# Loads of weights and context moved to one queue in the order of use, and a planner's figures redone, in a fused cross-attention and ternary feed-forward kernel

## The chip, the cores and the metric

The kernel runs on one core of a Trainium2 chip. The metric is the device time of one execution in microseconds (us). The engines are named as in the profile: PE (TensorE, with PEld for its weight loads), DVE (VectorE), ACT (ScalarE), POOL (GpSimd) and SP (SyncE, which here only issues DMAs). ACT can issue DMAs too, on a queue of its own. "ACTq" and "SPq" are the queue rows of the profile.

## The reference

```python
def xattn(query, key_value, mask, Wq, bq, Wk, bk, Wv, bv, Wo, bo):   # E=512, H=16, D=32
    Q, K, V = (each (. @ W.T + b), split in 16 heads of 32)
    scores = einsum('bqhd,bkhd->bhqk', Q, K) / sqrt(32)
    scores = where(mask == 0, -inf, scores)            # 77 keys per batch
    probs = softmax(scores)
    return einsum('bhqk,bkhd->bqhd', probs, V).reshape(B, Lq, E) @ Wo.T + bo

def ffn(x, w1, conv_w, conv_b, w2):                    # hidden 2048
    h = bit_linear(x, w1)        # x rounded to int8 per row, w to -1, 0, 1 by its mean |w|
    h = depthwise_conv1d(h, conv_w, conv_b)            # 3 taps along the sequence
    return bit_linear(silu(h), w2)

x = x + xattn(layernorm(x), ctx_1024, mask, ...)       # x: 4 x 2048 x 512 float32
x = x + ffn(layernorm(x), w1, conv_w, conv_b, w2)
```

## The kernel before

The 8192 rows of x are cut into 64 blocks of 128 rows. Two blocks make a pair, which shares its transposed input and its query products. For the feed-forward part the blocks are grouped into 18 tiles (`TILES`: two of 2 blocks, fourteen of 4, one of 3, one of 1).

**Start.** Wq, Wk, Wv and Wo (1 MB each), the transposed context (616 KB), the mask and the small columns are loaded into three buffers of the tag "y" (stage_A: wq and wv, stage_B: wk and mask, stage_C: wo and context). Wq and Wo are each split into two fp16 halves (a maximum on DVE, L436; high half on ACT, L441; low half on DVE, L446). The masked context gives keys (L525, first for batch 0, later for batches 1 to 3), the context gives values (L596). The value tiles (vx) lie in buffers of the tag "pr", which the exponentials use later; they are stored to DRAM (`vd`, L640), and the first batch's go to `vblk` by eleven small transfers (L665). W1 and w2 (4 MB each) are loaded in four pieces of 1 MB each (L751), summed for their mean (L756 on ACT, L761 on DVE), rounded (w_q, L781 and L783) and clipped to fp8. They reuse the three "y" buffers as stage_A to stage_C come free.

**One block.** Load x (L923), normalise (L853 to L879), split into two fp16 halves (hl: high half at L899 on ACT or L901 on POOL, low half at L930 on POOL), transpose by DMA (xT, L935). The query products (pq, L1212 to L1214) run per pair, a copy adds the bias (qT, L1222 on ACT). For each of four chunks of heads: scores (psc, L956, two PSUM buffers), maxima on DVE (L961), four exponentials on ACT (pr, L968). Per half of the heads: a cast (ph, L899), the low half on POOL (L993), a DMA transpose (prT, L997), value products (pa, L1005), scaling on DVE (L1022). Then the context is split and transposed (cT, L1058), multiplied by Wo (po, L1065 to L1070), added to x (xb, L1080), kept in DRAM, quantised and transposed (xqT, L1150).

**One tile.** For each of 16 chunks of the hidden width: product (ph, L1252), scaling (h, L1266, DVE), and the convolution's three taps. The middle tap is on ACT (L1277). A letter of `WHO[..]["conv"]` says who does the other two: "b" is both on DVE (L1292, into py and then into y), "c" is one on DVE and one on ACT plus POOL (ta at L1299, added at L1306), "d" is both on ACT plus POOL. SiLU follows on ACT (L1352), then maxima on DVE (L1357, L1393), then the rounding in pairs of chunks (gq, L1432, on POOL for "P" and on DVE for "D" in `WHO[..]["round"]`), the last product (pf, L1452), the residual (xr, L1462) and the store.

**The order.** All steps are given to a planner (`Plan.schedule`), which runs in Python before the kernel is built. Each step has an engine, a cost, a priority and, for DMAs, a latency and a time of service; the planner also reckons with eight DMA lanes, where each DMA waits for the one eight before it (`LANES`). The order that comes out is fixed for every engine at the end of the kernel (a chain of dependencies without semaphores), so every engine works strictly through its list. The figures of `O` and `LATER` are offsets in blocks that set the priorities, `PARTS` says at which block another set of figures and of `WHO` begins. In the order before, SP issues x of blocks 0 and 1, wq, wk, and ACT issues the columns, the context, the mask and wv; wo and bo follow on SP after the second transpose. All pieces of w1 and w2 are issued by ACT.

Of the kernel before, what the change touches and what calls it, by code (L numbers as in the profile page):

```python
# [17 lines left out]
I32 = mybir.dt.int32  # L18
# [6 lines left out]
P = 128  # L25
B, S, E = 4, 2048, 512
NK = 77
CK = B * NK
CG = (CK + P - 1) // P
H, D = 16, 32  # L30
# [40 lines left out]


O = {
    "first": -15.42, "pv": -17.5, "late": 1145.74, "w1": -8.83, "w2": 1.01, "k1": 5.45,
    "wo": -16.83, "bo": 1.54, "load": -3.75, "sa": -3.3, "na": 1.1, "hi": -8.89, "lo": -3.28,
    "xT": -3.9, "q": -1.76, "q_step": 0.36, "sc": -0.48, "sc_step": 0.02, "ph0": 0.05,
    "ph1": 0.92, "v0": -0.35, "v1": -3.13, "cx": 1.43, "o": 2.89, "n": 3.81, "xq": 3.53,
    "xb": -1.54, "h": 5.15, "s": 0.95, "p8": 0.63, "p8_step": 0.28, "f": 2.1,
}

LATER = [
    {"late": 958.43, "load": -3.97, "sa": -2.95, "na": 0.33, "hi": -7.55, "lo": -2.85,
     "xT": -3.83, "q": -1.75, "q_step": 0.42, "sc": -0.46, "sc_step": 0.0, "ph0": 0.04,
     "v0": -0.41, "v1": -1.84, "cx": 1.35, "o": 2.83, "n": 3.74, "xq": 3.23, "xb": -1.61,
     "h": 2.6, "p8": 0.62, "p8_step": 0.3, "f": 0.3},
    {"late": 1881.15, "load": -3.79, "sa": -2.94, "na": -1.29, "hi": -7.77, "lo": -2.51,
     "xT": -3.19, "q": -1.75, "q_step": 0.41, "sc": -0.49, "sc_step": 0.05, "ph1": 0.52,
     "v0": -0.87, "v1": -1.44, "cx": 1.53, "o": 2.82, "n": 3.92, "xq": 3.12, "xb": 1.12,
     "h": 4.4, "s": 0.99, "p8": 0.67, "p8_step": 0.32, "f": -0.11},
    {"late": 3023.22, "load": -3.22, "sa": -2.58, "na": -4.14, "hi": -7.03, "lo": -4.11,  # L90
     "xT": -2.17, "q": -1.66, "q_step": 0.39, "sc": -0.46, "sc_step": 0.12, "ph0": 0.17,
     "ph1": 1.1, "v0": 0.42, "v1": -0.26, "cx": 1.24, "o": 2.96, "n": 3.77, "xq": 3.89,
     "xb": -0.59, "h": 5.43, "s": 0.96, "p8": 1.12, "p8_step": 0.39, "f": -3.15},
]
SILU_ALL = False
COUPLE = False
# [6 lines left out]

PARTS = (12, 44, 54)
WHO = [
    {"sa": "D", "sf": "D", "xh": "A", "ch": "A", "ph": "AA", "q": "AAAA",
     "conv": "cbbbbbbbbbbbbcbb", "round": "PPPPPPPP"},
    {"sa": "D", "sf": "D", "xh": "P", "ch": "A", "ph": "AA", "q": "AAAA",  # L110
     "conv": "cbccbbcbbbbbbcbb", "round": "PPPPPPPP"},
    {"sa": "D", "sf": "D", "xh": "A", "ch": "A", "ph": "AA", "q": "AAAA",
     "conv": "cccbdbbbbbbbccbb", "round": "PPPPPPPP"},
    {"sa": "D", "sf": "D", "xh": "P", "ch": "A", "ph": "AA", "q": "ADAA",
     "conv": "ddbbbdcbbbbddcbb", "round": "PDPDPDPD"},
]


# [45 lines left out]
class Plan:  # L164
# [13 lines left out]
    def add(  # L178
        self, eng, cost, prio, uses, makes, fn, lock=False, table=None, lat=None, serve=0.0,
        delay=0.0, dmas=None,  # L180
    ):
        cost *= self.PACE.get(eng, 1.0)
        self.steps.append(
            Step(
                len(self.steps), eng, cost, prio, uses, makes, fn, lock, table,
                self.LAT[eng] if lat is None else lat, serve, delay,
                int(serve > 0) if dmas is None else dmas,
            )
        )
# [95 lines left out]
def xattn_bitffn_kernel(  # L285
# [15 lines left out]
    nc = tc.nc  # L301
# [24 lines left out]
    add = plan.add  # L326
# [34 lines left out]
    def square(name):  # L361

        s, i = {"wq": ("A", 0), "wv": ("A", 1), "wk": ("B", 0), "wo": ("C", 0)}[name]
        return st[s][:, EC * i : EC * i + EC]

    def tail(name, a, n):
        return flat(st[name])[:, EC * E + a : EC * E + a + n]
# [4 lines left out]
    def ctx_view():  # L372
        return by_chunk(tail("C", 0, EC * CK))

    def load_square(name, src, queue=nc.sync):
        queue.dma_start(out=square(name), in_=src.rearrange("(c p) o -> p c o", p=P))

    def load_ctx():
        nc.scalar.dma_start(out=small_in, in_=cols)
        nc.scalar.dma_start(out=ctx_view(), in_=ctxT.rearrange("(c p) k -> p c k", p=P))  # L380
        nc.scalar.dma_start(
            out=tail("B", 5 * CK, CK).bitcast(I32), in_=mask.partition_broadcast(P)
        )

    def load_o():
        nc.sync.dma_start(out=bo_f, in_=bo.partition_broadcast(P))
# [1 line left out]

    for s in "ABC":
        add("SP", 1, -41, [], {s: "y"}, partial(stage, s), lat=0)  # L390
    big = dict(lat=5000, serve=3000)
    add("SP", 450, -39.5, ["A"], {"wqd": None}, partial(load_square, "wq", wqT), **big)
    add("ACT", 1350, -39, ["B", "C"], {"ctxd": None}, load_ctx, dmas=3, **big)
    add(
        "ACT", 450, -37, ["A"], {"wv": None}, partial(load_square, "wv", wvT, nc.scalar),
        delay=1200, lat=4000, serve=3000,
    )
    add("SP", 450, -36.5, ["B"], {"wk": None}, partial(load_square, "wk", wkT), **big)
    add("SP", 900, -22, ["C", ("xTd", 1)], {"wo": None}, load_o, dmas=2, **big)


    p2 = {i: fixed([P, 1], F32, f"p2_{i}") for i in ("wq", "wo", "v")}
# [328 lines left out]
    def plan_ternary(dst, src, deq, name, prio):  # L731
# [9 lines left out]
            st[name, h] = new([P, G, TMAX], F32, "y", f"{name}_{h}")  # L741

        def load(i):
            h, k = divmod(i, 2)
            q = whole // 4
            if name == "w1":
                v = src[:, i * P : (i + 1) * P].rearrange("c p f -> p c f")
            else:
                v = src[i * E : (i + 1) * E].rearrange("(n p) f -> p n f", p=P)
            room = flat(st[name, h])[:, k * q : k * q + q]  # L750
            nc.scalar.dma_start(out=room.rearrange("p (c f) -> p c f", f=E), in_=v)  # L751

        def total(i):
            q = whole // 4
# [36 lines left out]
        for i in range(4):  # L791
            pr, w = prio + 0.3 * i, (name, i // 2)
            if i % 2 == 0:
                add("SP", 1, pr, W_GATE[name], {w: "y"}, partial(half, i // 2), lat=0)
            eng = "ACT" if (name, i) in SUM_ACT else "DVE"
            add(
                "ACT", 450, pr, [w], {(name, "l", i): None}, partial(load, i), lat=4000, serve=2500,
            )
            add(
                eng, 1890 if eng == "ACT" else 2195, pr, [w, (name, "l", i)],  # L800
                {(name, i, "t"): None}, partial(total, i),
            )
        add(
# [2 lines left out]
        )  # L806
        for i in range(whole // step):
            pr, q = prio + 1.3 + 0.1 * i, (name, "i", i)
            uses = [(name, "m"), (name, i * step * 2 // whole), (name, "l", i * step * 4 // whole)]
            eng, cost = ("ACT", 1050) if W_ROUND[name][i] == "A" else ("Pool", 1250)  # L810
            add(eng, cost, pr, uses, {q: "gq"}, partial(round_, i))
            add("DVE", 610, pr, [q], {(name, i, "q"): None}, partial(clip, i), lock=True)
# [99 lines left out]
    def plan_block(t):  # L912
# [25 lines left out]

        x, xn, hl, xT = (("x", t), ("xn", t), ("hl", t), ("xT", p))
        ahead = O["first"] + 0.3 * t if t < 2 else t  # L940
        early = -40 + 0.1 * t if t < 2 else t + O["load"]
        add("SP", 460, early, [], {x: "x"}, load, **LANDS["x"])
        both = pair.setdefault(p, {})
        plan_norm(
# [612 lines left out]
```

## Time and profile before

| what | value |
|---|---|
| time, median of 3 runs (lowest to highest) | 1199.87 us (1199.43 to 1202.67) |
| time of the profiled execution | 1198.85 us |
| its span, granted clock | 1197.0 us, 0.984 |
| busy PE / PEld / DVE / ACT / POOL | 1100.9 / 737.4 / 1075.2 / 951.0 / 955.6 us |
| DMA | 185.31 MB, mean 155 GB/s |
| queue q1 (issued by SP) | 173.49 MB |
| queue q10 (issued by ACT) | 10.27 MB |

The span is the profiled stretch from the first instruction to the last; the time of the execution is 1.85 us longer. Busy time counts an engine's instructions without register, branch, semaphore and DMA-issuing ones. In a row of a waits view the waiting line comes first, then the line that released it. A row of a timeline gives start and duration in us, then in brackets the idle time before it and what ended that.

### The profile page before, as it was taken

What the parts mean: (1) busy time and instruction counts of PE and PEld (TensorE: products, weight loads), DVE (VectorE), ACT (ScalarE), POOL (GpSimd) and SP (SyncE); (2) the same over time, 40 slices, a digit from 0 to 9 for tenths busy, and PEclk for the clock granted to TensorE, in tenths of its full rate; (3) what the DMA queues carried; (4) which work ended last, traced back from release to release, by engine and by line L of the source; (5) the groups of instructions that cost most, each with busy time, mean ns of one, the idle gap of its engine ahead of it and who ended that gap; (6) DMA issues with size and microseconds to landing.
All of it is one profiled execution on the core that took longest, in us unless ns stands there. A gap on an engine that the chain in (4) does not pass through costs nothing. (4 is left out here: it accounts for less than half of the span.)

```text
span 1197.0 us, 24157 instructions
## 1 busy us (share of the span) xinstructions
PE 1100.9 (92%) x8231; PEld 737.4 (62%) x8231; DVE 1075.2 (90%) x2380; ACT 951.0 (79%) x2124; POOL 955.6 (80%) x903
## 2 busy tenths in 40 slices
PE   4778889999999999999999999999999999997777
PEld 2455656766666676667676666666666766654333
DVE  4678789999999999999999999999999999899796
ACT  2478798888888888878888898979897988865563
POOL 4468759966978989797998889796989888788554
PEclk9889999999999999999999999999999999999899
DMA  7698986978676886858687777777686766651122
GB/s 229 168 288 164 194 183 151 195 137 177 117 168 135 168 188 143 173 127 185 138 174 164 175 159 167 156 147 163 150 171 154 169 133 154 131 145 54 40 71 88
DMA packets 396923, 185.31 MB, mean 155 GB/s; under 512 B 348107, under 2 KB 349259, under 8 KB 396799
## 3 DMA queue, kind: packets, MB, share of 16 engines
q1 hardware_dynamic: 391231, 173.49, 66.1%
q10 hardware_dynamic: 5568, 10.27, 2.6%
q8 instruction: 65, 1.06, 0.4%
q14 instruction: 59, 0.48, 0.1%
HBM read 64.97 MB, written 34.68 MB: 83 GB/s over the span
## 5 line engine op out<-in xcount | busy, mean ns | idle before, releaser
L1432 POOL TENSOR_TENSOR gq<-y,qsb 128x1024 f16<-128x1024 f32 (+3 forms) x132 | 289.6, 2212 | 10.0 <-ACT qsb L1410 5.3
L1252 PE MATMUL ph<-xqT,w1q 128*128 128x257 f16 (+3 forms) x2048 | 277.3, 276 | 15.0 <-DVE h L1266 12.7
L1277 ACT ACTIVATE py<-h,small_in 128x512 f32<-128x512 f32 (+3 forms) x270 | 202.5, 750 | 93.4 <-DVE y L1292 90.5
L968 ACT ACTIVATE pr<-psc,nmx 128x77 f32<-128x77 f32 x1024 | 245.7, 341 | 30.5 <-DVE nmx L961 27.0
L1452 PE MATMUL pf<-w2q,gq 128*128 128x512 fp8e4 x1024 | 260.5, 382 | 10.1 <-DVE xr L1462 5.7
L1252 PEld LDWEIGHTS <-w1q 128*128 128x128 fp8e4 x2048 | 199.2, 99 | 83.9 <-issue 32.1
L993 POOL TENSOR_TENSOR ph<-pr,ph 128x616 f16<-128x616 f32 x128 | 174.7, 1366 | 50.8 <-ACT ph L899 36.9
L1266 DVE TENSOR_TENSOR h<-ph,dqb 128x514 f32<-128x514 f32 (+3 forms) x288 | 180.2, 626 | 22.6 <-PE ph L1252 20.0
L1292 DVE SCALAR_TENSOR_TENSOR y<-h,small_in,py 128x512 f32<-128x512 f32 (+3 forms) x270 | 185.2, 686 | 1.9 <-ACT py L1277 1.0
L956 PE MATMUL psc<-kblk,qT 128*128 128x308 f32 x512 | 174.2, 437 | 11.4 <-ACT pr L968 10.7
L1306 POOL TENSOR_TENSOR y<-y,ta 128x512 f32<-128x512 f32 (+3 forms) x105 | 120.6, 1149 | 63.7 <-ACT ta L1299 36.6
L1452 PEld LDWEIGHTS <-gq 128*128 128x128 f16 x1024 | 98.0, 98 | 100.0 <-issue 14.6
L1357 DVE TENSOR_REDUCE mx<-y 128x256 f32<-128x2048 f32 (+2 forms) x66 | 146.0, 2213 | 11.8 <-ACT y L1352 11.6
L1212 PE MATMUL pq<-xT,wq_hi 128*128 128x256 f16 x512 | 142.1, 277 | 13.2 <-DMA xT<-hl 9.7
L1292 DVE SCALAR_TENSOR_TENSOR py<-h,small_in,py 128x512 f32<-128x512 f32 (+3 forms) x201 | 137.2, 682 | 8.7 <-ACT py L1277 8.2
L1213 PE MATMUL pq<-xT,wq_hi 128*128 128x256 f16 x512 | 142.2, 278 | 0.0
L1214 PE MATMUL pq<-xT,wq_lo 128*128 128x256 f16 x512 | 142.2, 278 | 0.0
L961 DVE TENSOR_REDUCE nmx<-psc 128x4 f32<-128x308 f32 x256 | 117.6, 468 | 13.1 <-PE psc L956 12.7
L1352 ACT ACTIVATE y<-y 128x2048 f32<-128x2048 f32 (+3 forms) x72 | 120.0, 1712 | 0.7 <-DVE y L1292 0.3
L956 PEld LDWEIGHTS psc<-kblk,qT 128*128 128x128 f32 x512 | 86.3, 191 | 41.3 <-ACT pr L968 23.8
L1005 PEld LDWEIGHTS <-prT 128*128 128x128 f16 (+1 forms) x1920 | 86.2, 98 | 37.2 <-DMA prT<-ph 18.1
L1005 PE MATMUL pa<-vblk,prT 128*128 128x66 f16 (+2 forms) x1920 | 92.4, 200 | 11.2 <-DMA prT<-ph 7.8
(158 smaller groups left out, 2022.2 us busy)
## 6 DMA issues: line engine op xcount, KB each, us to landing
x<-in_x SPq DMA_DIRECT2D x64, 256.0 KB
xb<-in_x SPq DMA_DIRECT2D x64, 256.0 KB
x<-xb SPq DMA_DIRECT2D x64, 256.0 KB
xr<-x SPq DMA_DIRECT2D x64, 256.0 KB
out<-xr SPq DMA_DIRECT2D x64, 256.0 KB
w<-in_w1T ACTq DMA_DIRECT2D x4, 1024.0 KB
w<-in_w2T ACTq DMA_DIRECT2D x4, 1024.0 KB
prT<-ph SPq DMA_TRANSPOSE x128
```

The costliest lines, as they stand in the source:

```text
L956: nc.tensor.matmul(psc, pair[p]["q", c][:, half], kb[:, c], start=True, stop=True)
L968: nc.scalar.activation(o["pr", c // 2][:, n : n + NK], o["psc", c][:, h], AF.Exp, bias=o["nmx", c][:, h : h + 1],)
L993: nc.gpsimd.tensor_tensor(ph[:, 1, :HR], o["pr", hf], ph[:, 0, :HR], ALU.subtract)
L1005: nc.tensor.matmul(pa[:, h0:h1], prT[:n, l + j], v[:, :, r], start=(j == 0 and i == 0), stop=(j == NS - 1 and i == 2), skip_group_check=True,)
L1213: nc.tensor.matmul(pq, hi[:, ic, os], xs[:, 1, ic], start=False, stop=False)
L1252: nc.tensor.matmul(ph[:, i, :WH], w1q[:, c, f * P : (f + 1) * P], xqT[:, c, c0 : c0 + WH], start=(c == 0), stop=(c == EC - 1),)
L1266: nc.vector.tensor_tensor(in_parts(s["h", f]), s["ph", f][:, :parts, :WH], in_parts(tile_a[a]["dqb"]), ALU.mult,)
L1277: nc.scalar.activation(dst, s["h", f][:, 1 : 1 + T], AF.Identity, bias=cb_sb[:, f : f + 1], scale=cw_sb[:, f, 1:2],)
L1292: nc.vector.scalar_tensor_tensor(ins[dst](), s["h", f][:, i : i + T], cw_sb[:, f, i : i + 1], ins[src](), ALU.mult, ALU.add,)
L1357: nc.vector.tensor_reduce(s["m", g][:, c0:c1], ys[g][:, :, c0:c1].rearrange("p c t i -> p t c i"), AX.XY, ALU.max, apply_absolute_value=True,)
L1432: engine.tensor_tensor(gq[u][:, :, :T], y, q, ALU.mult)
L1452: nc.tensor.matmul(s["po", k], gq[f // 2][:, f % 2, k * P : (k + 1) * P], w2q[:, f], start=(f == 0), stop=(f == HC - 1),)
```

## The change

Three things change. (1) Wq, the columns, the context, the mask, wk, wv and all pieces of w1 and w2 are issued by SP, in the order of their use; ACT issues no DMA any more. (2) W1 and w2 come in eight pieces of 512 KB each, where they came in four of 1 MB; the sums wait for two pieces, a rounding waits for one. (3) The planner's latencies for these loads, all offsets in `O` and `LATER`, the boundaries `PARTS` and the assignment `WHO` are new. In `WHO`, the first chunk of a tile goes from "c" to "d" in the first three parts, one rounding of the third part goes from POOL to DVE, the third part's high half of hl goes from ACT to POOL, and the last part's conv and round letters are arranged anew (as many chunks with DVE taps: 20 taps on DVE, four pair roundings on DVE).

```diff
-    "first": -15.42, "pv": -17.5, "late": 1145.74, "w1": -8.83, "w2": 1.01, "k1": 5.45,
-    "wo": -16.83, "bo": 1.54, "load": -3.75, ...
+    "first": -14.87, "pv": -18.61, "late": 1061.05, "w1": -8.76, "w2": -2.26, "k1": 3.07,
+    "wo": -12.87, "bo": -5.67, "load": -5.34, ...
...
-PARTS = (12, 44, 54)
+PARTS = (12, 48, 56)
 WHO = [
     {"sa": "D", "sf": "D", "xh": "A", "ch": "A", "ph": "AA", "q": "AAAA",
-     "conv": "cbbbbbbbbbbbbcbb", "round": "PPPPPPPP"},
+     "conv": "dbbbbbbbbbbbbcbb", "round": "PPPPPPPP"},
     {"sa": "D", "sf": "D", "xh": "P", "ch": "A", "ph": "AA", "q": "AAAA",
-     "conv": "cbccbbcbbbbbbcbb", "round": "PPPPPPPP"},
-    {"sa": "D", "sf": "D", "xh": "A", "ch": "A", "ph": "AA", "q": "AAAA",
-     "conv": "cccbdbbbbbbbccbb", "round": "PPPPPPPP"},
+     "conv": "dbccbbcbbbbbbcbb", "round": "PPPPPPPP"},
+    {"sa": "D", "sf": "D", "xh": "P", "ch": "A", "ph": "AA", "q": "AAAA",
+     "conv": "dccbdbbbbbbbccbb", "round": "PPPDPPPP"},
     {"sa": "D", "sf": "D", "xh": "P", "ch": "A", "ph": "AA", "q": "ADAA",
-     "conv": "ddbbbdcbbbbddcbb", "round": "PDPDPDPD"},
+     "conv": "ddbdbdbbbbbddbbb", "round": "DDPPPDPD"},
 ]
...
-        nc.scalar.dma_start(out=small_in, in_=cols)
-        nc.scalar.dma_start(out=ctx_view(), in_=ctxT.rearrange("(c p) k -> p c k", p=P))
...
+        nc.sync.dma_start(out=small_in, in_=cols)
+        nc.sync.dma_start(out=ctx_view(), in_=ctxT.rearrange("(c p) k -> p c k", p=P))
...
-    big = dict(lat=5000, serve=3000)
-    add("SP", 450, -39.5, ["A"], {"wqd": None}, partial(load_square, "wq", wqT), **big)
-    add("ACT", 1350, -39, ["B", "C"], {"ctxd": None}, load_ctx, dmas=3, **big)
-    add(
-        "ACT", 450, -37, ["A"], {"wv": None}, partial(load_square, "wv", wvT, nc.scalar),
-        delay=1200, lat=4000, serve=3000,
-    )
+    big = dict(lat=2300, serve=2900)
+    add("SP", 450, -39.8, ["A"], {"wqd": None}, partial(load_square, "wq", wqT), **big)
+    add("SP", 1350, -39.7, ["B", "C"], {"ctxd": None}, load_ctx, dmas=3, lat=2300, serve=2500)
     add("SP", 450, -36.5, ["B"], {"wk": None}, partial(load_square, "wk", wkT), **big)
-    add("SP", 900, -22, ["C", ("xTd", 1)], {"wo": None}, load_o, dmas=2, **big)
+    add("SP", 450, -36.4, ["A"], {"wv": None}, partial(load_square, "wv", wvT), **big)
+    add("SP", 900, -22, ["C", ("xTd", 1)], {"wo": None}, load_o, dmas=2, lat=2300, serve=3600)
...
         def load(i):
-            h, k = divmod(i, 2)
-            q = whole // 4
+            h, k = divmod(i, 4)
+            q = whole // 8
...
-            nc.scalar.dma_start(out=room.rearrange("p (c f) -> p c f", f=E), in_=v)
+            nc.sync.dma_start(out=room.rearrange("p (c f) -> p c f", f=E), in_=v)
...
+            for j in (2 * i, 2 * i + 1):
+                add(
+                    "SP", 450, pr, [w], {(name, "l", j): None}, partial(load, j), lat=2000,
+                    serve=1450,
+                )
             add(
-                "ACT", 450, pr, [w], {(name, "l", i): None}, partial(load, i), lat=4000, serve=2500,
-            )
-            add(
-                eng, 1890 if eng == "ACT" else 2195, pr, [w, (name, "l", i)],
+                eng, 1890 if eng == "ACT" else 2195, pr,
+                [w, (name, "l", 2 * i), (name, "l", 2 * i + 1)],
                 {(name, i, "t"): None}, partial(total, i),
             )
...
-        early = -40 + 0.1 * t if t < 2 else t + O["load"]
+        early = -40 + 0.5 * t if t < 2 else t + O["load"]
```

In the order that the planner gives for the changed kernel, SP begins with x of block 0, wq, the columns, the context, the mask, x of block 1, wk, wv. Then come x loads and the first two transposes, bo, wo, the first four pieces of w1, the first transpose of the second pair, three reloads of x, the value stores and the vblk loads with the other four pieces of w1 among them, the second transpose of the second pair, and the two batches of w2 with transposes before and between them. On PE the key products of batch 0 come before all value products, and the scores of the first pair come before the queries of the second.

## The prediction

> **What bounds the kernel now.** I first cut the profiled execution (span 1197.0 us, time 1198.85) into stages, because the change touches the first 90 us and the order of everything after. The table by stage: stretch, its length, then busy time of PE, PEld, DVE, ACT, POOL, granted clock, DMA share, GB/s.
> ```profile
> 0.00:16.00 16.00, 0.18 (x1) 0.21 (x2) 7.12 (x19) 2.52 (x3) 10.22 (x24) 1.00 0.89 301
> 16.00:38.00 22.00, 22.00 (x108) 13.38 (x108) 11.84 (x29) 8.64 (x14) 11.27 (x15) 1.00 0.57 148
> 38.00:66.00 28.00, 19.82 (x91) 13.39 (x89) 16.42 (x42) 14.29 (x30) 11.56 (x15) 0.82 0.78 207
> 66.00:132.00 66.00, 53.26 (x369) 33.27 (x369) 54.30 (x121) 52.56 (x159) 50.48 (x50) 0.92 0.92 217
> 300.00:1060.00 760.00, 745.12 (x5809) 513.62 (x5807) 719.43 (x1570) 650.36 (x1457) 664.54 (x586) 1.00 0.72 156
> 1060.00:1197.00 137.00, 104.34 (x573) 54.82 (x570) 110.34 (x200) 77.19 (x117) 84.38 (x78) 0.94 0.24 73
> ```
> From 300 to 1060 us PE is busy 98% and DVE 95%: there only less work on these two, or a better fit of their waits, can pay. PE idles 15.8 us before 16, none until 38, then 8.2 and 12.7 us up to 132, and 32.7 us in the last stage. So loads can matter up to 132. Who waits there is in the waits of 38 to 132 us (waiting line, releaser, total us, times, longest), and the reason in the timeline of SP's and ACT's queues (start, duration).
> ```profile
> PEld psc L956 <- ACT pr L968: 13.0, 13, 2.4
> ...
> PE psc L956 <- ACT pr L968: 6.9, 8, 1.6
> ...
> PE pq L1212 <- DMA xT<-hl: 5.0, 1, 5.0
> ```
> ```profile
> 36.92 1.48 SPq L935 DMA_TRANSPOSE xT<-hl  x1
> ...
> 45.62 0.33 SPq L640 DMA_DIRECT2D vd<-vx  x1
> ...
> 51.10 9.62 SPq L665 DMA_DIRECT2D vblk<-vx  x9
> ```
> ```profile
> 58.09 1.91 ACTq L751 DMA_DIRECT2D w<-in_w1T  x2
> 60.10 0.97 ACT L968 ACTIVATE pr<-psc,nmx 128x77 f32<-128x77 f32 x4 [1.67 <-DMA vblk<-vx]
> ```
> PE waits for exponentials (L968). The first of them starts at 60.10 although its maxima were done at 41.3: ahead of it in ACT's order stand four query copies, which waited for a transpose that took from 36.92 to 48.9, and the two issues of w1's second half, which wait at 58 to 60 for the small vblk transfers (at most eight DMAs are in flight: each waits for the one eight before).
>
> **The change, part by part.** The costs come from these groups (count | busy, mean ns of one | idle before); three more rows give 742 ns for a DVE tap into py, 1218 for a pair rounding on DVE and 740 for a 256-wide addition on POOL.
> ```profile
> L1432 POOL TENSOR_TENSOR gq<-y,qsb 128x1024 f16<-128x1024 f32 x108 | 259.2, 2415 | 4.7 <-PE pf L1452 4.7
> ...
> L1292 DVE SCALAR_TENSOR_TENSOR y<-h,small_in,py 128x512 f32<-128x512 f32 x216 | 159.7, 739 | 1.5 <-ACT py L1277 1.0
> ...
> L1306 POOL TENSOR_TENSOR y<-y,ta 128x512 f32<-128x512 f32 x77 | 100.0, 1298 | 35.7 <-ACT ta L1299 16.3 <-DVE y L1292 14.8 <-ACT pr L968 3.1
> ...
> L901 POOL TENSOR_SCALAR hl<-xn_xn 128x512 f16<-128x512 f32 x42 | 26.0, 620 | 6.9 <-DMA xT<-hl 5.6
> ```
> *Up to 38 us.* Wq now goes second, so its maximum (13.40 before) can start near 7. But PE's first long work is now the key product, which needs wk and the masked context. Ahead of wk and with it lie 3.4 MB on one queue; at the 301 GB/s of the first stage that is 11.5 us, plus some 2.5 us until the first bytes land (x is there at 3.69): 14. The context chain on DVE (wq maximum 2.28, mask work 1.5, scales 1.7, mean and mask 1.6, a norm 1.0, from the mask's arrival, 9.5 now as before) ends near 15.5. PE starts at 15.6 against 15.82 and has the same products, 21.7 us (16 to 38 is full), before the first scores: 37.3 against 37.5. Worth 0.2; between 3 us better (wk early) and 2 us worse (cold start on other matmuls).
>
> *38 to 75 us.* The load of wo and bo moves behind both first transposes and an x, from 18.08 to about 28, and w1's first half is issued when the value products have left their buffer, near 32 (37.5 before). The sum of w1's first quarter now stands ahead of the value halves on ACT, and the wo maximum ahead of the value scale on DVE; so the value tiles are stored at about 45.5, as before (45.62): no gain yet. Then the chains part. ACT no longer issues DMAs, nor has the second pair's query copies in front of the exponentials; the first exponential waits for the second value store only. That is issued after one store and three vblk loads (46.0 to 48.84 in SP's rows) and takes some 2.5 us without w1 beside it: 51.5 against 60.10, 8.6 us earlier. Block 0's eight plus eight exponentials (0.97 to 1.04 per four), the two casts (0.80) and the key copies put the first transposes of probabilities near 62, and the first value product near 65.5 against 74.04. Against this: the second pair's second transpose goes from place 17 on SP to place 45, behind 8 pieces of w1, three stores and eleven vblk loads; at the 1.07 us per vblk row (9.62/9) and 0.45 per piece it is issued near 61 (36.92 before), lands near 64, and the second pair's queries run at 64 to 69 (48.9 to 59 before). They are needed for the ninth score product, at about 73 before; 5 us of lead are left there. W1's mean, at 72.48 before, comes near 66. W2's eight pieces can follow at about 68 to 72 (74.79 to 76.91 before). I take 5 us, the tightest of these leads; ends 0 and 8.6. Sixteen pieces for eight loads cost SP 8 issues of 0.45 more, and twelve issues leave ACT, 5.8 us by their rows; both beside other work, except the two at 58 that are counted already.
>
> At this place the queue itself is the doubt. The row: the transpose issued at 36.92, on a queue of its own beside 2 MB of w1 on ACT's, was waited for until 48.90. So two queues did not protect it.
> The Trainium skill ("DMA: Bandwidth & Descriptors", Issuing engines are not separate DMA queues) says that DMAs from different engines run on the same 16 engines, and that issuing from several saves only issue time; its section on queues, rings and completion order adds that an engine takes turns between queues packet by packet. By that, nothing is gained in bandwidth by one queue, and a transpose behind four pieces waits for all of their 2 MB. With the first rule alone the sum would be only the 0.2 us and ACT's issues. No run here shows the taking of turns by itself.
>
> *From 132 us.* In the order of the changed kernel, PE's instructions are the same in number and kind. Counting the forms on the others: DVE has 13 full taps into y fewer and 2 into py more (-13 x 0.739 + 2 x 0.742), two 256-wide fewer, two roundings more (2 x 1.218), one query copy fewer: -7.0 us with the short forms. POOL has 11 full and 2 short additions more (11 x 1.298 + 2 x 0.740), 10 casts more (10 x 0.620), two roundings fewer (-2 x 2.415): +17.2 us. ACT is within 1 us. DVE's 7.0 lie on the engine that is 95% busy, but PE beside it is at 98%, so I count 3 (ends 0 and 7). POOL's 17.2 are hidden by its own idle time, 95 us from 300 to 1060; without that cover they would end in roundings (gq), then in PE's last products, and cost up to 17. The planner's new numbers also reorder steps everywhere, in the tail too, where PE idles 32.7 us; taps and roundings there are the same in number, 4 pair roundings stay on DVE per tile. I price this at 0, with 4 us either way.
>
> Sum: -5 - 3 = -8 on the span of 1197.0, so 1189; with the 1.85 us around it 1190.85; the median of the runs shown is 1.0 above that execution, so 1192.
>
> **The rivals.** *The lead is lost before it counts.* Between 66 and 132 us DVE, ACT and PE are each about 80% busy and chained to each other, POOL too; if the chain of blocks rather than its start sets when the hidden products begin (132.5 now), or if DVE's relief only turns into PE waits, the result is within 3.6 us of now: 1199. For it speaks that PE's waits for exponentials (13.0 + 6.9) are spread over 21 times.
>
> *One queue holds back the transposes.* SP waits in order for buffers and for the DMA eight before. If w1's second half has to wait for its buffer until the wo split is done (49.5 before, 51.8 by my count, 5 more if wo lands late), everything behind it, the second pair's transpose above all, slips to 72 or more; the ninth score is then 5 us late instead of 5 early. W2's two batches stand before transposes as well; at the gaps of w2's landings, 2.7 to 3.1 us per MB, each batch of 2 MB adds 5.8 us to a transpose behind it, and one of them is then no longer hidden. Together +10.8, less 3 of DVE: 1207. The point from which it decides is that transpose's issue: at 61 a gain, beyond 70 a loss. Against it: before, too, transposes lay in a hole while w2 came (none issued between 71.06 and 84.93).
>
> **How the numbers follow.** My forecast, faster: 0.66, its own range 1183 to 1196. Lead lost: 0.12. One queue holds back: 0.22, from 1204 to 1212. The measurement tells about 0.3% from no change, 3.6 us. The lower end 1181 takes in the full 8.6 plus the full 7 and some of the tail; the upper end 1206 leaves out the worse half of the last case, about 0.1.
>
> **What would show it.** Right: the first L968 row near 51.5 and no issue on ACT's queue; first value product near 66; first hidden product (ph) near 127; DVE's busy sum 7 us lower and POOL's 17 higher, with PE's share from 300 to 1060 unchanged or higher. Wrong: exponentials at 58 or later; the second pair's transpose issued after 70, or PE waiting for xT; waits of pf for POOL's gq growing from 3.2 us; a last stage longer than 141 us.

## The result, and the profile after

Slower by 5 us, where a gain of 8 was forecast: 1205.36 us (median of 7 runs, 1203.11 to 1207.45) against 1200.37 us of the kernel before in the same comparison; ratio 1.0046, 95% interval 1.0028 to 1.0065. The profiled execution took 1204.06 us, its span is 1202.2 us, the granted clock 0.981. Forecast were 1192.0 us, 1181 to 1206. That the time lies inside this range is no merit of the sum: its upper end was drawn for the last of the rivals, not for the case that was forecast.

Lines of the kernel after stand up to five lower than the same lines before (L525 is L520, L956 is L955); in the experiments they shift again. The table by stage of the kernel after (columns as in the prediction: stretch, length, busy PE, PEld, DVE, ACT, POOL, granted clock, DMA share, GB/s):
```profile
0.00:16.00 16.00, 0.83 (x3) 0.60 (x4) 8.70 (x28) 3.90 (x3) 7.80 (x22) 1.00 0.87 295
16.00:38.00 22.00, 22.00 (x94) 14.36 (x94) 7.50 (x17) 6.46 (x12) 15.86 (x17) 1.00 0.46 120
38.00:66.00 28.00, 15.81 (x58) 11.07 (x56) 20.11 (x46) 14.66 (x33) 12.64 (x12) 0.76 0.89 258
66.00:132.00 66.00, 51.27 (x386) 35.18 (x386) 50.44 (x108) 46.91 (x136) 46.87 (x45) 0.87 0.85 197
...
300.00:1060.00 760.00, 744.46 (x5823) 514.27 (x5821) 717.38 (x1547) 657.05 (x1468) 680.73 (x605) 1.00 0.72 156
1060.00:1202.20 142.20, 111.51 (x645) 59.84 (x643) 123.15 (x231) 80.98 (x127) 88.54 (x82) 0.96 0.30 84
```
From 300 to 1060 us PE is busy for as long as before (744.46 against 745.12). The loss is ahead of that: from 38 to 66 us PE is busy 4.0 us less and runs at a clock of 0.76 instead of 0.82, from 66 to 132 us at 0.87 instead of 0.92. The first hidden product (ph) comes at 141.0 us; it came at 132.5, and 127 was forecast.

The waits of 38 to 132 us show two that were not there before:
```profile
PE pk L520 <- DVE rs_xn L865: 11.1, 1, 11.1
...
PE psc L955 <- ACT pr L967: 6.5, 5, 2.3
...
PE pa L1004 <- DMA prT<-ph: 4.7, 1, 4.7
```
The first in the timelines of PE and of DVE, after a line of PE before the change:
```profile
48.90 0.37 PE L1212 MATMUL pq<-xT,wq_hi 128*128 128x256 f16 x1 [4.99 <-DMA xT<-hl]
```
```profile
43.64 1.88 PE L690 MATMUL pb_o<-stage_C,small_in 128*128 128x512 f32 x4
56.62 3.42 PE L520 MATMUL pk<-stage_B 128*128 128x231 f32 x8 [11.10 <-DVE rs_xn L865]
```
```profile
48.51 2.26 DVE L757 TENSOR_REDUCE part_w<-w 128x1 f32<-128x2048 f32 x1
...
50.69 2.33 DVE L441 SCALAR_TENSOR_TENSOR wo_lo<-stage_C,s_wo,wo_hi 128x2048 f16<-128x2048 f32 x1
52.95 0.68 DVE L696 TENSOR_TENSOR bo_f<-pb_o,bo_f 128x512 f32<-128x512 f32 x1
...
54.90 1.58 DVE L513 TENSOR_TENSOR stage_B<-stage_B,kblk 128x924 f32<-128x924 f32 x1
```
PE's next instruction from 45.5 us on is the key product of batches 1 to 3. It needs the masked context (L511, L513), which is done at 56.48; the row names the short DVE instruction right behind it. In DVE's list these two stand behind the sum of w1, the low half of wo and the bias row, and come at 53.64. Before the change PE did the second pair's queries here (48.9 to 59). These now stand behind all key products in PE's list and run from 69.9 to 78.1; the pair's second transpose is issued only at 60.37.

The second in SP's timeline:
```profile
60.37 1.29 SPq L934 DMA_TRANSPOSE xT<-hl  x1
...
70.12 1.93 SPq L747 DMA_DIRECT2D w<-in_w2T  x4
...
74.02 4.49 SPq L996 DMA_TRANSPOSE prT<-ph  x1
79.05 3.12 SPq L747 DMA_DIRECT2D w<-in_w2T  x4
82.28 3.23 SPq L934 DMA_TRANSPOSE xT<-hl  x1
```
A transpose of probabilities, issued behind four pieces of w2, lands 9.9 us later (83.95; landings here and below are read from the DMAs' semaphore records in the trace); the third pair's first transpose stands behind the other four and lands at 90.2. The third pair's queries run at 99.4 (76.1 before).

From some 3 us into each of the two stretches PE's granted clock is at half, from 48.0 to 61.7 and from 82.1 to 95.8 us:
```profile
48.00:61.70 13.70, 5.08 (x12) 4.19 (x13) 10.04 (x19) 4.61 (x13) 10.35 (x9) 0.50 0.69 233
82.10:95.80 13.70, 8.46 (x39) 4.51 (x40) 12.64 (x18) 5.59 (x19) 9.25 (x9) 0.50 1.10 287
112.90:116.30 3.40, 3.40 (x12) 1.77 (x11) 2.42 (x7) 2.87 (x11) 2.02 (x2) 0.50 0.37 90
```
The Trainium skill ("TensorE: Matmul & The Clock Gate", HAM oscillation) says that idle gaps of PE of more than about 3.4 us put its clock to half. This trace agrees for the stretches of 11.1 and 4.7 us. But the clock is at half from 112.9 to 116.3 us too (last line), and PE's longest idle stretch in the 7 us ahead of that is 2.3 us; before the change it was at half from 74.2 to 81.0 us, after idle stretches of at most 1.4 us. So the length of a single gap does not decide alone.

### The profile page after: what moved, and what is told of

It reads as the page before. It is cut to its first block, busy times and chain, and to the rows that moved or that the text cites. A ratio compares the mean times of both kernels' runs of the same rounds, so it can differ in the third digit from the quotient of the medians.

```text
span 1202.2 us, 24138 instructions
## 1 busy us (share of the span) xinstructions
PE 1099.8 (91%) x8231; PEld 741.3 (62%) x8231; DVE 1076.3 (90%) x2368; ACT 955.4 (79%) x2128; POOL 978.6 (81%) x924
## 4 chain that ended last, share of the span: by engine, by line
PE 25%; DVE 24%; POOL 21%; ACT 12%; DMA 8%; issue 8%; SPq 2%; POOLq 0%; DVEq 0%; ACTq 0%
POOL gq L1431 7%; PE ph L1251 5%; PE pf L1451 5%; DVE y L1291 4%; POOL ph L992 3%; DVE mx L1356 3%; DVE h L1265 3%; DVE py L1291 3%; ACT y L1351 3%; PE psc L955 3%; DMA prT<-ph 3%; ACT pr L967 2%; PE pa L1004 2%; POOL y L1305 2%; DMA xT<-hl 2%
## 5 line engine op out<-in xcount | busy, mean ns | idle before, releaser
L1431 POOL TENSOR_TENSOR gq<-y,qsb 128x1024 f16<-128x1024 f32 (+3 forms) x130 | 285.1, 2209 | 10.8 <-ACT qsb L1409 10.8
L1276 ACT ACTIVATE py<-h,small_in 128x512 f32<-128x512 f32 (+3 forms) x253 | 189.6, 749 | 90.6 <-DVE y L1291 81.4
L1305 POOL TENSOR_TENSOR y<-y,ta 128x512 f32<-128x512 f32 (+3 forms) x118 | 136.6, 1158 | 68.1 <-ACT ta L1298 58.9
L955 PE MATMUL psc<-kblk,qT 128*128 128x308 f32 x512 | 175.4, 442 | 10.7 <-ACT pr L967 10.1
L1291 DVE SCALAR_TENSOR_TENSOR y<-h,small_in,py 128x512 f32<-128x512 f32 (+3 forms) x253 | 173.4, 685 | 4.3 <-ACT py L1276 2.7
L1356 DVE TENSOR_REDUCE mx<-y 128x256 f32<-128x2048 f32 (+2 forms) x66 | 145.9, 2213 | 6.0 <-ACT y L1351 5.8
L1211 PE MATMUL pq<-xT,wq_hi 128*128 128x256 f16 x512 | 139.6, 273 | 5.8 <-DMA xT<-hl 3.0
L1213 PE MATMUL pq<-xT,wq_lo 128*128 128x256 f16 x512 | 139.5, 273 | 0.0
L1212 PE MATMUL pq<-xT,wq_hi 128*128 128x256 f16 x512 | 139.5, 272 | 0.0
L955 PEld LDWEIGHTS psc<-kblk,qT 128*128 128x128 f32 x512 | 88.4, 194 | 38.4 <-ACT pr L967 20.0
```

The source lines that it names most:

```text
L955: nc.tensor.matmul(psc, pair[p]["q", c][:, half], kb[:, c], start=True, stop=True)
L1276: nc.scalar.activation(dst, s["h", f][:, 1 : 1 + T], AF.Identity, bias=cb_sb[:, f : f + 1], scale=cw_sb[:, f, 1:2],)
L1291: nc.vector.scalar_tensor_tensor(ins[dst](), s["h", f][:, i : i + T], cw_sb[:, f, i : i + 1], ins[src](), ALU.mult, ALU.add,)
L1305: nc.gpsimd.tensor_tensor(y, y, s["ta", f, i][:, :T], ALU.add)
L1356: nc.vector.tensor_reduce(s["m", g][:, c0:c1], ys[g][:, :, c0:c1].rearrange("p c t i -> p t c i"), AX.XY, ALU.max, apply_absolute_value=True,)
L1431: engine.tensor_tensor(gq[u][:, :, :T], y, q, ALU.mult)
```

## The experiments

The theories: **F**, the order of the front (up to the first hidden product) costs the time; **M**, the new division of work and order behind it; **Q**, the one queue itself; **X**, order and figures are fitted to each other as a whole, so that any single step away from them costs. The expectations name further ones for their own runs: P is that the places in the list cost and not the queue, T1 to T3 put the loss in one of three stretches, A and B are about one move. The median of the kernel before lay between 1198.7 and 1200.5 us in all comparisons. "First ph" is the first hidden product in the profiled run.

**Code and figures apart.** e2_loads is the changed kernel with the old `O`, `LATER`, `PARTS` and `WHO`; e3_figures the old kernel with the new ones; e4_x1 the changed one with `early = -40 + 0.1 * t`, that is, block 1's x second on the queue, as before.

> The new load code (one queue, pieces of 512 KB, new latencies) with the old figures, PARTS and WHO. Its order up to the first hidden product is nearly that of the changed kernel: the second pair's second transpose stands behind the vblk loads, the later batches' key products stand ahead of the scores. Theory F (the loss is made in the front by that order): first hidden product again near 141 us instead of 132.5, PE idle about 11 us near 45 to 57, time 1203 to 1209. Theory M (the loss is made by the new split of work and the figures, POOL's 17 us more): time at or below that of the kernel before, 1192 to 1200.

> The old load code with the new figures, PARTS and WHO. The front keeps the old order. Theory F: first hidden product within 3 us of 132.5, time 1194 to 1201, since the last stage of the changed kernel gave back about 3 us. Theory M: 1203 to 1208, with the loss growing between 300 and 1060 us.

> The changed kernel with one number put back: x of block 1 is loaded second again (-40 + 0.1 t instead of -40 + 0.5 t). The planner then has block 1's transpose early, puts the first pair's queries between the value products, and the second pair's queries ahead of the later batches' key products. Theory F: no PE hole of 11 us, first hidden product near 130 to 135, time 1194 to 1201. Theory M: the front may change but the time stays at 1203 to 1208.

Measured: 1218.96 (1.0158, 1.0134 to 1.0181), 1226.33 (1.0235, 1.0205 to 1.0265) and 1228.70 us (1.0251, 1.0229 to 1.0273). All the numbers expected were missed: each mixture loses 20 to 29 us on the kernel before in the same comparison, more than the change itself. A figure is an offset that makes the planner order 5,900 steps, so one figure (0.1 for 0.5) gives another order in all parts of the list. These runs say that the new figures go with the new loads, and nothing on where the 5 us are lost. From here on the planned list is taken as it stands and single steps are moved in it by hand, so that the rest stays.

**Single moves in the changed kernel's list.**
```diff
 s3_mask   + move([("ctx", 1)], behind=("vl", 2))                  # mask work ahead of w1's sum on DVE
 s4_pair   + move([("xTd", 3)], behind=("xTd", 2))                 # second pair's transposes together
           + move([("pq", 1, 0), ("pq", 1, 1)], ahead=("e", 0, 0)) # and its queries ahead of the keys
           + ...  # the other queries and their copies, the bias row, two scores and a cast to fit
 s5_w2     + move([("w2", "l", j) for j in range(4)], behind=("prT", 1, 0))
           + move([("w2", 1)] + [("w2", "l", j) for j in range(4, 8)], behind=("xTd", 4))
 s7_all    + the three together
 s8_pairs  + s3 and s4, and ("xTd", 4), ("xTd", 5) ahead of w2's loads, ("pq", 2, ...) among block 2's scores
```


> The changed kernel with its planned list of steps kept as it is and one step moved by hand: the masking of the context for batches 1 to 3 (DVE) goes right behind the value halves, ahead of w1's second sum, the wo half and the bias row. Theory F (the loss is made in the front, by PE's idle stretch from 45.5 to 56.6 us, by its wait for prT at 79 to 84 us and by the half clock that follows each): the key products start near 50 to 52 instead of 56.6, the idle stretch shrinks from 11.1 to about 5 us, the first hidden product comes 2 to 4 us before 141, time about 1202. Theory M (the loss is made from 132 us on, by the new split of work, POOL's 17 us above all): the hole shrinks and the time stays at 1205. Theory X (order and figures are fitted to each other as a whole, and any move away from them costs): 1208 or more.

> The changed kernel with its planned list, but the second pair's second transpose goes right behind its first on SP, and the second pair's query products and copies go into PE's idle stretch, ahead of the key products of batches 1 to 3, with two score products among them (as before the change). Theory F: the query products of pair 1 run at about 48 to 58 us instead of 69.9 and later, PE's busy time up to 66 us rises by some 5 us, the half clock after the hole is shorter, the first hidden product comes 3 to 5 us before 141, time about 1201. Theory M: the front fills and the time stays at 1205. Theory X: 1208 or more.

> The changed kernel with its planned list, but w2's first four pieces go behind the transpose of block 1's first probabilities on SP, and its second four behind the third pair's first transpose. Theory F: that transpose lands about 6 us after its issue at the latest instead of 9.9, PE's wait of 4.7 us at 79 to 84 is gone, the half clock from 82 to 96 is shorter, time about 1202. Theory M: the wait goes and the time stays at 1205. Theory X: w2's rounding comes 4 us later and the hidden products with it, 1208 or more.

> The three moves of s3_mask, s4_pair and s5_w2 together on the changed kernel's list. Theory F: both idle stretches gone, PE's work done by 300 us back to about 250 us (243.9 after, 251.4 before), first hidden product at 132 to 136, time 1195 to 1199, at or below the kernel before. Theory M: PE's work by 300 us rises as well, but it is given back between 300 us and the end, time 1203 to 1206. Theory X: 1208 or more.

> The changed kernel's list with the moves of s3_mask and s4_pair, and the third pair's two transposes put ahead of w2's loads on SP (with the halves of block 5 that they need), its query products among the scores of block 2 on PE (73 to 90 us instead of 99 and later, as before the change at 76 to 90). Theory P: both idle stretches are filled with work that has to be done anyway, the first hidden product comes at 134 to 137 instead of 141, time 1196 to 1200. Theory M (the loss is made from 132 us on): the front fills but the time stays at 1203 to 1206. Theory X (any move from the planned order costs): 1208 or more.

| kernel | time, us | ratio, interval | first ph |
|---|---|---|---|
| after | 1205.36 | 1.0046, 1.0028 to 1.0065 | 141.0 |
| s3_mask | 1204.54 | 1.0038, 1.0018 to 1.0058 | 140.8 |
| s4_pair | 1203.69 | 1.0035, 1.0018 to 1.0052 | 139.5 |
| s5_w2 | 1208.11 | 1.0061, 1.0042 to 1.0081 | 142.9 |
| s7_all | 1208.27 | 1.0072, 1.0048 to 1.0097 | 143.8 |
| s8_pairs | 1209.88 | 1.0082, 1.0062 to 1.0103 | 145.0 |

The moves did locally what they should: in s3_mask the wait falls from 11.1 to 6.0 us, in s4_pair PE is busy 23.57 us from 38 to 66 (15.81 after), in s5_w2 the value product that waited 4.7 us runs at 78.6 instead of 84.0. No gain in time came of it that can be told. In s3_mask and s4_pair the value product behind w2's pieces still waits 5.2 and 5.7 us for its transpose, and what s4_pair does ahead of 66 us is in part missing behind it (PE busy 46.92 us from 66 to 132, 51.27 after). For the moves of w2, s7_all shows why; its DVE and ACT:
```profile
82.94 2.29 DVE L757 TENSOR_REDUCE part_w<-w 128x1 f32<-128x2048 f32 x1 [1.39 <-DMA w<-in_w2T]
86.08 2.29 DVE L757 TENSOR_REDUCE part_w<-w 128x1 f32<-128x2048 f32 x1 [0.85 <-DMA w<-in_w2T]
```
```profile
88.86 1.83 ACT L967 ACTIVATE pr<-psc,nmx 128x77 f32<-128x77 f32 x8 [8.34 <-DVE nmx L960]
```
W2's pieces land later, DVE stands before their sums, the maxima stand behind these in DVE's list, ACT waits 8.34 us for them and PE 9.08 for ACT. The wait had only gone to the next list. By the times set down beforehand F's (in s8_pairs P's) were missed in all five runs; s3_mask and s4_pair lie at M's 1205, s5_w2, s7_all and s8_pairs at X's 1208 or more. As F's sign was a first hidden product some us earlier, and none came more than 1.5 us earlier, F was neither shown nor refuted by these runs; X does not hold for each single step.

**The queue alone.** On the old planned list, s1_queue issues everything on SP, s2_queue512 also cuts the pieces; s6_actq puts w1 and w2 back on ACT's queue in the changed kernel's list.
```diff
 s1_queue      -  nc.scalar.dma_start(...)   (four places)
               +  nc.sync.dma_start(...)
 s2_queue512   +  and two DMAs of 512 KB where there was one of 1 MB
 s6_actq       -  nc.sync.dma_start(out=room..., in_=v)
               +  nc.scalar.dma_start(out=room..., in_=v)
```


> The kernel before with its planned list untouched; only the engine that issues the loads of weights and context is changed from ACT to SP, at the same places of the list and with the same 1 MB pieces. Theory P (places: what costs is where the new plan puts transposes, mask work and pair queries, not the queue): no measurable change, 1197 to 1203. Theory Q (one queue: a transpose behind bulk loads on the same queue waits for all of their bytes, and that makes the loss): the change's own loss or more, 1204 to 1210, with PE waiting for prT or xT behind w1 and w2.

> As s1_queue, and each of the eight 1 MB loads of w1 and w2 cut into two of 512 KB issued one after the other at the same place. Theory P: as s1_queue within 2 us; eight issues of 0.45 us more on SP are hidden. Theory Q: as s1_queue or up to 3 us worse, since SP is held 3.6 us longer and at most eight DMAs are in flight.

> The changed kernel with its planned list untouched; only the sixteen pieces of w1 and w2 are issued by ACT again, at the same places of the list. Theory P: the loss stays, 1203 to 1207, since the idle stretch at 45 to 57 us and the late pair queries stay; ACT's exponentials come up to 2 us later. Theory Q: most of the loss goes, 1198 to 1202, and the wait for prT at 79 to 84 us with it.

Measured: 1197.10 us (0.9982, 0.9966 to 0.9998), 1199.11 (0.9987, 0.9972 to 1.0002) and 1212.01 (1.0110, 1.0078 to 1.0142). Q falls: one queue alone is no loss, and in s1_queue a gain of some 2 us, whose interval just excludes no change; taking w1 and w2 off it in the changed kernel costs 7 us more. P's times hold for the first two runs and not for s6_actq (1203 to 1207 expected). SP in s1_queue:
```profile
37.75 1.49 SPq L935 DMA_TRANSPOSE xT<-hl  x1
39.35 0.89 SPq L751 DMA_DIRECT2D w<-in_w1T  x1
```
The transpose goes first and w1 stands behind it (its two pieces are issued 1.6 and 3.3 us later); it lands 5.4 us after its issue. In the kernel before it lands after 11.9 us, with w1's 2 MB issued on ACT's queue 0.6 us later. The second pair's queries start at 44.7 instead of 48.9, the first hidden product at 129.8. The other way round s6_actq shows it:
```profile
PE pa L1004 <- DMA prT<-ph: 10.5, 1, 10.5
```
The transpose of probabilities issued at 74.5 lands 15.7 us later beside w2 on ACT's queue; on one queue, behind four pieces and ahead of the other four, it took 9.9. There w2's second four pieces are issued 2.2 to 4.8 us behind the transpose, and two of them land ahead of it all the same (88.4 and 90.1). So in these places a transpose was held up little by what was issued behind it on its own queue, and much by what was issued behind it on another. The times of the runs hold more than that: the loads' issues leave ACT's list or come back to it as well. In s1_queue the first exponential starts at 54.77 instead of 60.10, in s6_actq it waits 5.0 us for a vblk transfer (2.9 us for a store after); no run parts this from the queue. S1_queue has the lowest median of all versions tried, but its interval overlaps those of s2_queue512 and h1_front.

**Front and rest crossed.** The old and the new plan have almost the same steps ahead of the first hidden product (493 and 509: eight pieces of w1 and w2 more by the cut, and eight other steps). h1_front is the changed kernel with these steps in the old order; h2_front is s2_queue512 with them in the new order.
```diff
-    for s in plan.schedule():
+    for s in weave(plan, FRONT):   # steps of FRONT in that order, then the others as planned
```


> The changed kernel (one queue, 512 KB pieces, its own division of work), but the 493 steps that the old plan puts ahead of the first hidden product run in the old plan's order; all steps after them in the changed kernel's. Theory F (the loss lies in the order of the first 130 us): first hidden product at 130 to 133 instead of 141, time 1195 to 1199; the 3 us that the last stage gave back are kept, so it may lie below s2_queue512. Theory M (it lies in the order and division after 130 us): first hidden product early as well, but the lead is given back by the end, 1203 to 1206.

> The cross of it: the kernel s2_queue512 (old plan, one queue, 512 KB pieces), but the 509 steps that the changed kernel's plan puts ahead of the first hidden product run in that order; the rest in the old plan's. Theory F: idle stretch of 11 us at 45 to 57, first hidden product near 141, time 1205 to 1210. Theory M: first hidden product late as well, but the time 1197 to 1201.

| | old rest | new rest |
|---|---|---|
| old front | s2_queue512: 1199.11 (0.9987) | h1_front: 1198.16 (0.9984, 0.9967 to 1.0001) |
| new front | h2_front: 1207.68 (1.0067, 1.0045 to 1.0088) | after: 1205.36 (1.0046) |

This settles it for F, as the order of the front in the whole, and against M: the new front costs 7 to 9 us with either rest, the new rest nothing that can be told. Both times lie where F had put them. From 16 us to the first hidden product in s2_queue512, then in h2_front:
```profile
16.00:130.40 114.40, 92.64 (x578) 60.72 (x579) 82.88 (x193) 75.91 (x201) 73.74 (x81) 0.96 0.84 209
```
```profile
16.00:141.70 125.70, 98.03 (x593) 65.21 (x593) 83.86 (x189) 75.75 (x206) 79.11 (x82) 0.89 0.77 193
```
For nearly the same products (15 short ones more) PE is idle 5.9 us longer (27.67 against 21.76) and busy 5.4 us longer, at a clock of 0.89 instead of 0.96: nearly half of the delay between these two goes with the clock. Between the kernel before and the one after it is otherwise:
```profile
16.00:132.50 116.50, 95.58 (x578) 60.54 (x578) 83.06 (x193) 75.53 (x201) 73.81 (x82) 0.91 0.82 202
```
```profile
16.00:141.00 125.00, 96.88 (x593) 65.28 (x593) 84.33 (x190) 75.97 (x207) 81.80 (x83) 0.88 0.78 194
```
PE is idle 7.2 us longer there and busy 1.3 us longer, since before the change, too, its clock was at half in parts of this stretch (from 46.9 to 57.1 us, for one). So of the 8.5 us by which the change is late, most is idle time. S2_queue512 and h2_front have the same list from there on, and the delay of 11.3 us goes through to the end of these two profiled runs: 10.5 to 12.4 us at the other tiles' first products, 11.7 at the last product of the second layer (the medians of all runs differ by 8.6).

**Which stretch of the front.** As h1_front, with the old order up to the first score product, up to the first value product, and from there on only.

> As h1_front, but only the 93 steps that the old plan puts up to the first score product (37 us) run in the old order; all others in the changed kernel's. If the start decides (T1: block 1's x and transpose early again): 1197 to 1201. If 38 to 74 us decides (T2) or 74 to 130 us (T3): 1203 to 1207.

> As h1_front, but the old order only up to the first value product (74 us; by then the old plan has the third pair's transposes and none of w2's loads, the new one four of w2's loads and none of these transposes); after it the changed kernel's. T1 and T2: 1196 to 1200. T3: 1203 to 1207.

> The cross: the changed kernel's order up to the first value product, then the old order up to the first hidden product, then the changed kernel's again. T1 and T2: the loss is made by then and stays, 1204 to 1209. T3: 1196 to 1201.

Measured: 1207.05 (1.0054, 1.0034 to 1.0074; first ph 143.9), 1201.82 (1.0024, 1.0007 to 1.0040; 141.0) and 1214.03 us (1.0124, 1.0106 to 1.0141; 145.9). The start decides nothing (T1 falls). The rest does not add up, and h4_to74 and h5_from74 both missed every time expected: the old order up to 74 us seems to win back half, but its first hidden product comes no earlier, and the cross to it is slower than either kernel.

**One move of the new order in the old one**, on s2_queue512.
```diff
 g1_pair3  + ("xTd", 4) behind ("w2", "l", 3); ("xTd", 5) behind ("prT", 2, 0); ("pq", 2, ...) behind ("psc", 3, 3)
 g2_pair2  + ("xTd", 3) behind ("kv", 0, 3); ("ctx", 1) behind "bo"; ("pq", 1, ...) behind ("pk", 3, 1)
```


> s2_queue512 (old plan, one queue, 512 KB pieces) with one thing as in the changed kernel: the third pair's two transposes stand behind w2's loads and behind the transpose of block 2's first probabilities on SP, and its query products behind the scores of block 3. Theory A (any pair whose queries come late takes away the work that fills PE between two blocks; PE idles and then runs at half clock): 1202 to 1206, granted clock in the front 0.90 or less (0.96 in s2_queue512), first hidden product at 134 to 139. Theory B (only the whole new order costs): 1198 to 1201.

> s2_queue512 with one other thing as in the changed kernel: the second pair's second transpose stands behind the loads of block 0's values, the masking of the context for batches 1 to 3 behind w1's second sum, the wo half and the bias row on DVE, and the second pair's query products behind all key products. Theory A: an idle stretch of PE of 8 to 11 us at 45 to 57 us and half clock after it, 1204 to 1209. Theory B: 1198 to 1201.

Measured: 1220.49 us (1.0178, 1.0158 to 1.0198; first ph 151.9) and 1216.44 (1.0147, 1.0127 to 1.0167; 146.6). Both dearer than theory A had it, and dearer than the whole change. The third pair's transpose in g1_pair3 on SP, and what ACT does:
```profile
67.73 5.30 SPq L852 DMA_DIRECT2D w<-in_w2T  x8
73.07 5.03 SPq L1036 DMA_TRANSPOSE xT<-hl  x1
```
```profile
83.35 0.62 ACT L1000 CAST hl<-xn_xn 128x512 f16<-128x512 f32 x1 [8.33 <-DMA xT<-hl]
```
The transpose lands behind all of w2, 10 us after its issue. It holds the buffer hl, a cast of ACT waits for that buffer, and the exponentials behind the cast wait with it: PE waits 30.9 us for them between 38 and 140 us, where it waits 12.3 in s2_queue512. The changed kernel has the same late transposes and loses less; that its list has the casts and the other pairs placed for them is likely, but was not tested. In g2_pair2 the hole is there (9.9 us for stage_B), and 17.1 us of waits for exponentials.

**What joins the runs** is the first hidden product. With the new rest: 131.9 us in h1_front gives 1198.16, 141.0 after gives 1205.36, 145.0 in s8_pairs 1209.88, 146.9 in s6_actq 1212.01: 13.9 us of time for 15.0 us of start. With the old rest: 129.8 in s1_queue gives 1197.10, 141.7 in h2_front 1207.68, 151.9 in g1_pair3 1220.49: 23.4 us for 22.1. The other runs lie within 2.2 us of the straight lines between these ends, but for h4_to74 (141.0, 1201.82), 4.7 us below, and h5_from74 (145.9, 1214.03), 2.9 above, which stays open.

## Why the prediction was wrong

**What held.** The first exponential starts at 52.33 us (51.5 forecast, 60.10 before), the value tiles are stored at 46.97 (45.5), ACT issues nothing, the second pair's second transpose is issued at 60.37 and lands at 64.3 (61 and 64). The key products started at 15.61 (15.6). That the start of the hidden products goes through to the end, nearly us for us, held too: the runs of the last paragraph have it at 0.9 to 1.1, h4_to74 and h5_from74 apart. From 300 to 1060 us PE's busy sum is unchanged within 0.7 us.

**The step that failed** is "5 us of lead", under 38 to 75 us: not a lead but a delay of 8.5 us at the first hidden product. Its leads were gone by 72 to 74 us, though the exponentials came 7.8 us early:
```profile
72.28 0.71 PE L1004 MATMUL pa<-vblk,prT 128*128 128x66 f16 x15 [0.25 <-DVE mean_w L766]
72.83 0.76 PE L955 MATMUL psc<-kblk,qT 128*128 128x308 f32 x2
```
The first value product starts 1.8 us before its old time (74.04) and not 8.5, the ninth score product stands at about its old time (73) and not 5 us ahead, w1's mean (72.07) is 0.4 us early and not 6. The step failed in three places.
- The prediction followed exponentials and transposes, and asked of the second pair's queries only whether they came in time for the ninth score. They came at 69.9, in time for the scores of block 2 (72.8). But they had also been what PE did between 48.9 and 59 while it waited for other things. Moved away, they left the hole of 11.1 us; the work next in PE's list hung on three DVE steps that the sum never named, and the queries were then done where the value products and scores should have been early.
- The third pair was not looked at. Its transposes went behind w2's pieces in the same way, its queries from 76.1 to 99.4.
- The clock had no term. From 16 us to the first hidden product PE's clock is 0.88 after, 0.91 before and 0.96 in s2_queue512.

That the order of the front makes the loss is shown by the crosses. How much of it each place makes is not: filling the hole alone (s4_pair) brought the first hidden product 1.5 us forward, and filling it together with an early third pair (s8_pairs) put it 4.0 us back.

**Smaller misses.** The first score products came at 39.24 us, not at 37.3 (37.31 before): the key products of batch 0, first on PE now, took 7.08 us, where they took 3.84 behind value products. H3_to38, which puts them at 37.72, gains nothing by it. And ahead of the first exponential before the change stood three query copies (52.03, 55.29, 57.95), not four; the fourth follows at 60.94.

**The rivals.** "One queue holds back the transposes" gave 1207 and the right sign, and much of its mechanism was there: each batch of w2 stood before a transpose, and one of the waits was not hidden (4.7 us, 5.8 priced). But its point of decision was the wrong one: the transpose named was issued at 60.37, where a gain was foretold. And it is not the queue that does it, but the place in the order: with the old order the queue gains. "The lead is lost" had the first exponentials early without a gain, but gave 1199.

**The term of the queue** had the wrong sign as well. "Nothing is gained in bandwidth by one queue" is so, but the row that the prediction read (36.92 to 48.90 for a transpose beside 2 MB on another queue) was itself the cost that one queue takes away: 11.9 to 5.4 us. It was read as "two queues did not protect it" and not followed to its end. What of this reached the time is small (some 2 us in s1_queue), and ACT's freed list has a part in it. The Trainium skill ("DMA: Bandwidth & Descriptors", Issuing engines are not separate DMA queues) says that several issuing engines save only issue time; the runs agree in that one queue loses nothing (0.9982 and 0.9987 of the time before), and show that a second one can delay a small transfer. Its section on queues, rings and completion order, that a DMA engine takes turns between queues, fits the 11.9 and 15.7 us; no run shows the turns themselves.

**The 3 us of DVE relief** did not come. The instructions were counted rightly: the durations of DVE's instructions sum to 1232.9 us after 1239.1 (6.2 less, 7.0 forecast), and POOL's forms named in the sum rise by 17.6 us (17.2 forecast). But the time in which DVE is busy at all, overlapping instructions counted once, rises from 1075.2 to 1076.3 us, and with the same front the new rest gives 0.9984 against 0.9987. This prices DVE's relief, POOL's added work and the tail's reordering together, at nothing that can be told; each by itself was not measured, and the intervals leave room for some 2 us.

## What to carry to other kernels

Before moving a transfer, list what the bottleneck engine does in the time around it, and ask of each piece of work that moves away what that engine's next instruction is then and which list that hangs on; in g2_pair2 moving a filler away cost 17 us, more than the hole of 9.9 us that it left. Put a transfer that is waited for on the same queue ahead of the bulk, neither behind it nor beside it on another queue, as far as these runs go. In a list that a planner has fitted, test one cause by freezing the list, and cross the parts of two whole lists: single repairs here only moved the wait to another place.

## What the runs showed of the hardware

A small transfer that was issued first took 5.4 us with 2 MB issued behind it on its queue (1.6 and 3.3 us later) and 11.9 us with the same 2 MB issued on another queue 0.6 us later; this was not expected to matter. A second case goes the same way: 15.7 us with four pieces of w2 issued 2.2 to 4.8 us later on another queue, against 9.9 on one queue. PE's clock was at half for 13.7 us around the hole of 11.1 us, the last 5.1 of them with PE at work again; and it fell to half after idle stretches of 2.3 and 1.4 us as well.
